# Group norm, a quantised 3x3 convolution and a residual on one core: 31 images in the direct form and 122 in the combined form in place of 75 and 82, with the engines' order taken from a timetable

## The chip, the cores and the metric

The kernel runs on one core of a Trainium2 chip. The time is the device time of one execution in microseconds (us). The core's engines each have a queue of their own and meet through semaphores: TensorE (PE: matmuls into PSUM; PEld is its weight load), VectorE (DVE), ScalarE (ACT), GpSimd (POOL) and SyncE (SP), which only issues DMAs here. GpSimd issues DMAs too. Each engine works strictly in the order in which its instructions were emitted.

## The reference

`x` has 160 images of 128 channels, 32 by 32, float32; `U` has five sets of weights (128 by 128 by 9). The reference, cut to what matters:

```
gn(x)  = (x - mean) / sqrt(var + 1e-5)          # per image and group of 4 channels
s1 = (max(U) - min(U)) / 3;  v1 = s1 * floor(U / s1)
s2 = s1 / 5;                 v2 = s2 * floor((U - v1) / s2)
w  = v1 + v2                                    # 5 sets
out = x + conv3x3(gn(x) of images 32n..32n+31, w[n], padding 1)   # n = 0..4
```

The normalised image is carried as two float16 parts, a high part and the rest (low part), and the weights, being small whole numbers after scaling, fit in float16.

## The kernel before, in words

One image fills the core's 128 partitions (a channel each) with 1,024 elements. Images are worked on in order, 0 to 159, and set `n` of the weights serves 32 of them. There are three forms of an image's convolution, counted here in matmuls of up to 512 columns, which is what TensorE spends:

- **Direct** (images 0 to 2): high and low part each go through 9 taps into 2 row parities, 36 matmuls.
- **Mixed** (75 images): the high part goes through the 9 taps for both parities (18 matmuls, `taps`). The low part is first turned on VectorE into sums and differences of row pairs (`combinations`, three operations), and then needs 12 matmuls (`product`): 30 in all.
- **Combined** (82 images): the sums and differences are built of the image itself into a wide tile `v` of 2,048 columns: on GpSimd the outer columns and the last quarter (`beside_pairs`), on VectorE the rest (`combine`, two operations). ScalarE scales it to the high part `vh`, VectorE makes the low part `vl` of 2,048 columns. Both go through `product`: 24 matmuls.

For mixed and combined images the sums of pairs come out of two passes, `m2` and `m1` (`sums_of_pairs`, 6 matmuls in a mixed image and 12 in a combined one, within the counts above). ScalarE copies `m2` out of PSUM (`leave`), VectorE makes both PSUM halves of the result from `m1` and `m2` (`pairs`, two operations), and the `main` matmuls add onto them. TensorE's order is: the sums of image i+1, then `main` of image i in two halves. There is one `m2` place, two `m1` places, and two pairs of result banks.

The result leaves PSUM by ScalarE (`sum<-eo`) and is added to the image in SBUF by an accumulating DMA that GpSimd issues (`accumulate`); for every eighth image and the last four VectorE does both in one operation (`by_hand`). SP stores two images at a time and loads the next two into the same place; there are 11 places of two images.

Statistics: for each image ScalarE runs two activations with accumulators (a sum, then a square about the mean, `measure`); eight images ride on VectorE instead (`BY_VECTOR`). For groups of images (2, 2, 4, 4, 4, 4, 4, then eight at a time) a float32 matmul averages over channel groups, VectorE forms the deviations, a second matmul averages them, ScalarE, GpSimd (a power) and VectorE finish the scale. From `z` on: a mixed image is normalised on GpSimd (`z`; the first of each group on ScalarE), cut to `hi` on ScalarE and to `lo` on VectorE.

The weights of sets 1 to 4 are quantised during the images before them, a third of a set (a column of taps) at a time: 14 VectorE operations of 384 elements a column (`quantise`, line 112 on), a transposing matmul and a ScalarE copy (`keep_taps`), and at the end sums of taps (`sums_of_set`).

The order is written out by hand in `run`: for each image a fixed list of calls, with a rule for every kind of image, measuring 14 images ahead and loading 18 ahead. GpSimd's operations get an extra wait for the last VectorE operation before `pairs`, so that they run while VectorE reads PSUM:

```
def combined(self, i):
    if i < self.STEADY or i >= self.imgs: return False
    if i < self.FIFTHS: return i % 2 == 1
    return (i - self.FIFTHS) % 5 % 2 == 0 if i < self.THIRDS else i % 3 != 1
```

Here `STEADY` is 7, `FIFTHS` 126 and `THIRDS` 146: every other image is combined at first, then three in five, at the end two in three.

Of the kernel before, what the change touches and what calls it, by code (L numbers as in the profile page):

```python
# [16 lines left out]
N_SETS = 5  # L17
# [13 lines left out]
WIDEST = 40.0  # L31


class Steps:
# [61 lines left out]
    def nearest(self, pool, v, parts, name, dt, by_scalar=False):  # L96

        tag = "m" if by_scalar else "nn"
        n = pool.tile(list(v.shape), dt, tag=tag, name=f"n{tag}_{name}")
        engine = self.nc.scalar.mul if by_scalar else self.nc.vector.tensor_scalar_mul  # L100
        return n, engine(n, v, parts[0])
# [13 lines left out]
    def quantise(self, pool, un, name, dt, by_scalar=False):  # L115
# [14 lines left out]
        nn, first = self.nearest(pool, rest, self.parts2, name + "_2", ints)  # L130
# [215 lines left out]
class Main:  # L346
# [24 lines left out]
    STAT_LEAD = 14  # L371
    LOAD_LEAD = 18
    STEADY = 7
    BY_VECTOR = (8, 10, 11, 14, 19, 24, 29, 34)
    FIFTHS = 126
    THIRDS = 146
# [9 lines left out]
    def __init__(self, tc, ctx, keep, x, u, out):  # L386
# [17 lines left out]
        self.xpool = pool("x", 11)  # L404
        self.zpool = pool("z", 3)
        self.parts = pool("parts", 5)
        self.rows = pool("rows", 4)
        self.wide = pool("wide", 2)
        self.wide_parts = pool("wide_parts", 3)
# [3 lines left out]
        self.small = pool("small", 3)  # L413
# [14 lines left out]
        self.sum = {}  # L428
        self.tables, self.wts, self.across = {}, {}, {}
        self.columns = []  # L430

        cuts = [0, 2, 4, 8, 12, 16, 20, *range(24, self.imgs + 1, 8)]
# [143 lines left out]
    def measure(self, i, stages=(0, 1)):  # L576
# [8 lines left out]
        for s in stages:  # L585
            junk = self.unread.tile([self.P, 1024], MM, tag="junk", name=f"junk{i}_{s}")
            (st.image_sum, st.image_square)[s](j, image, junk)

    def normalise(self, i):
# [3 lines left out]
        z = self.zpool.tile([self.P, 1024], F32, tag="z", name=f"z{i}")  # L593
# [11 lines left out]
    def combined(self, i):  # L605

        if i < self.STEADY or i >= self.imgs:
            return False

        if i < self.FIFTHS:  # L610
            return i % 2 == 1
        return (i - self.FIFTHS) % 5 % 2 == 0 if i < self.THIRDS else i % 3 != 1

    def by_scalar_too(self, i):

        return i < self.FIRST + 4 or i == self.groups[self.group_of[i]].start
# [21 lines left out]
    def combine(self, i):  # L638
# [4 lines left out]
        v, x, half = self.v[i], self.image(i), self.W // 2  # L643
# [11 lines left out]
    def beside_pairs(self, i, after):  # L655

        nc = self.nc
        if self.combined(i):
            self.v[i] = self.wide.tile([self.P, 2048], F32, tag="v", name=f"v{i}")
            self.after(self.outer_columns(i), after)  # L660
            even, odd = (self.image(i)[:, a::2] for a in range(2))
            ins = nc.gpsimd.tensor_sub(self.v[i][:, 1536:], odd, even)  # L662
        elif self.by_scalar_too(i):
            return
        else:
            st, j = self.column_of(i)
            z = self.z[i] = self.zpool.tile([self.P, 1024], F32, tag="z", name=f"z{i}")
            ins = nc.gpsimd.tensor_scalar(  # L668
                z, self.image(i), st.ngm[:, j], st.rstd[:, j], ALU.add, ALU.mult
            )  # L670
        self.after(ins, after)

    def after(self, ins, before):

        self.tc.add_manual_dep(
            ins.ins, before.ins.name,
# [44 lines left out]
    def taps(self, i, part, col, target, parities=(0, 1)):  # L721
# [7 lines left out]
        for k in self.KS:  # L729
            for a in parities:  # L730
# [7 lines left out]
                    start=(i < self.FIRST and col == self.COLS[0] and k == 1 and top == 0),  # L738
# [54 lines left out]
    def m1(self, i):  # L793
        return self.m1b if i % 2 else self.m1a
# [5 lines left out]
    def sums_of_pairs(self, i):  # L800

        for quarter, kind, target in (
            (3, self.DIFF, self.m2_ps), (2, self.SUM, self.m1(i))
        ):
            for step in self.KS:
                self.product(target, i, quarter, step, kind, start=step == self.KS[0])

    def conv(self, i, on_the_way):


        if self.FIRST < i < self.imgs - 1:
            self.sums_of_pairs(i + 1)
        if i == self.FIRST:
            self.main(i, 0)
            on_the_way(self.COLS[1])
            self.sums_of_pairs(i + 1)
            self.main(i, 1)
# [405 lines left out]
```

## Time and profile before

| | us |
|---|---|
| three runs | 978.17, 979.36, 985.92 (median 979.36) |
| the profiled execution | 982.18 |
| its span, first to last instruction | 980.5 |
| TensorE busy | 943.3 (96%) |
| VectorE busy | 913.8 (93%) |
| ScalarE busy | 833.4 (85%) |
| GpSimd busy | 353.5 (36%) |
| granted TensorE clock | 0.997 |

Busy time is the time in which at least one instruction of the engine was under way. The instructions of an engine overlap a little at their ends: an operation listed with 2.34 us lets the next one start after 2.26. A table by stage cuts the span into stretches and gives each engine's busy time in them; the difference to the length of the stretch is idle. The table of waits says who idled for whom.

### The profile page before, as it was taken

Reading aid. Unit: us, or ns where it says so; the run is one execution under the profiler, and the core shown is the slowest. Engines: PE = TensorE matmul, PEld = TensorE weight load, DVE = VectorE, ACT = ScalarE, POOL = GpSimd, SP = SyncE. Lnnn points to the kernel's source line nnn. Section 1 sums busy time; section 2 is a strip of 40 time slices with the busy share of each in tenths; the row PEclk is TensorE's granted clock in tenths of the full one; section 3 lists DMA queues with packets and bytes.
Section 4 is the critical chain, followed back from the end, with each engine's and each line's share of the span. In section 5 each row is a group of like instructions: output and inputs, shape, how many; then the busy total and the mean of one; then the engine's idle time right before and its main releaser. Section 6 shows DMA issues by size and latency. Waiting matters only on the chain.

```text
span 980.5 us, 13236 instructions
## 1 busy us (share of the span) xinstructions
PE 943.3 (96%) x4504; PEld 440.8 (45%) x4504; DVE 913.8 (93%) x1332; ACT 833.4 (85%) x1135; POOL 353.5 (36%) x441
## 2 busy tenths in 40 slices
PE   2899999999999999999999999999999999999997
PEld 1444444444444444444444444444444444444443
DVE  7999999998999999899999998799999998989995
ACT  5779889999999999889898989698989899898551
POOL 4353333343333333333343333233433434333530
PEclk9999999999999999999999999999999999999999
DMA  9627889999998888999998999998989989998774
GB/s 352 264 95 207 230 236 267 265 250 257 319 297 242 269 232 244 257 289 273 250 267 240 272 247 253 285 281 265 239 261 259 258 249 269 247 247 251 178 207 160
DMA packets 65117, 245.86 MB, mean 251 GB/s; under 512 B 5008, under 2 KB 5008, under 8 KB 65040
## 3 DMA queue, kind: packets, MB, share of 16 engines
q1 hardware_dynamic: 45312, 173.09, 49.4%
q0 software_dynamic: 19728, 71.84, 38.8%
q8 instruction: 37, 0.61, 0.2%
q14 instruction: 40, 0.33, 0.1%
HBM read 89.19 MB, written 83.89 MB: 177 GB/s over the span
## 4 chain that ended last, share of the span: by engine, by line
PE 74%; DVE 12%; DMA 6%; issue 4%; ACT 2%; POOL 2%; SPq 0%; DVEq 0%; POOLq 0%
PE eo L789 25%; PE eo L734 23%; PE m L789 12%; PE m1b L789 8%; PE m1a L789 5%; DMA out_dram<-xt 3%; DVE vl L690 2%; DVE v L644 1%; DMA u<-in_L_conv_U_dram 1%; DVE lo L697 1%; DVE eo L846 1%; DMA xt<-sum 1%; DMA range<-in_L_conv_U_dram 1%; DVE eo L848 1%; DVE v L651 1%
## 5 line engine op out<-in xcount | busy, mean ns | idle before, releaser
L734 PE MATMUL eo<-hi,wt 128*128 128x496 f16 (+2 forms) x1386 | 367.7, 375 | 0.7 <-ACT wt L527 0.7
L789 PEld LDWEIGHTS <-wt 128*128 128x128 f16 x1884 | 183.9, 99 | 216.1 <-DVE rows L719 5.2
L734 PEld LDWEIGHTS <-wt 128*128 128x128 f16 x1458 | 142.6, 99 | 163.7 <-ACT wt L527 1.4
L874 ACT COPY sum<-eo 128x1024 f32<-128x1024 f32 x137 | 143.1, 1045 | 63.2 <-PE eo L789 63.0
L690 DVE SCALAR_TENSOR_TENSOR vl<-v,rstd,vh 128x2048 f16<-128x2048 f32 x82 | 192.2, 2344 | 1.4 <-ACT vh L684 1.4
L789 PE MATMUL eo<-vh,wt 128*128 128x496 f16 (+1 forms) x492 | 185.0, 376 | 1.0 <-DVE eo L848 0.9
L789 PE MATMUL eo<-vl,wt 128*128 128x496 f16 (+1 forms) x492 | 184.9, 376 | 0.0
L684 ACT ACTIVATE vh<-v,rstd 128x2048 f16<-128x2048 f32 x82 | 164.1, 2001 | 17.1 <-DVE v L651 16.9
L209 ACT ACTIVATE junk<-xt,mv 128x1024 f16<-128x1024 f32 x152 | 174.3, 1147 | 0.1
L202 ACT ACTIVATE junk<-xt 128x1024 f16<-128x1024 f32 x152 | 160.6, 1057 | 15.2 <-DMA xt<-in_x_dram 11.6
L789 PE MATMUL eo<-rows,wt 128*128 128x496 f16 (+1 forms) x450 | 170.8, 380 | 0.0
L789 PEld LDWEIGHTS <-across 128*128 128x128 f16 x984 | 96.2, 98 | 116.0 <-issue 5.1
L668 POOL TENSOR_SCALAR z<-xt,ngm,rstd 128x1024 f32<-128x1024 f32 x53 | 62.8, 1184 | 232.3 <-DVE tt L109 39.6
L632 POOL TENSOR_SCALAR v<-xt,ngm 128x64 f32<-128x64 f32 x82 | 30.9, 377 | 257.1 <-issue 72.7
L897 POOL DMA_DIRECT2D xt<-sum x137 | 119.8, 878 | 4.4 <-ACT sum L874 3.1
L837 ACT ACTIVATE m<-m 128x512 f32<-128x512 f32 x157 | 94.0, 599 | 24.9 <-PE m L789 18.7
L644 DVE TENSOR_TENSOR v<-xt 128x960 f32<-128x960 f32 x82 | 106.2, 1295 | 2.8 <-POOL v L632 2.8
L789 PE MATMUL m<-vl,across 128*128 128x496 f16 (+1 forms) x246 | 92.1, 374 | 3.3 <-DVE vl L690 3.2
L697 DVE TENSOR_TENSOR lo<-z,hi 128x1024 f16<-128x1024 f32 x78 | 94.9, 1216 | 0.0
L789 PE MATMUL m<-vh,across 128*128 128x496 f16 (+1 forms) x246 | 92.1, 375 | 0.0
L662 POOL TENSOR_TENSOR v<-xt 128x512 f32<-128x512 f32 x82 | 84.8, 1034 | 0.0
L602 ACT CAST hi<-z 128x1024 f16<-128x1024 f32 x78 | 81.5, 1044 | 1.2 <-POOL z L668 0.5
(144 smaller groups left out, 1151.8 us busy)
## 6 DMA issues: line engine op xcount, KB each, us to landing
xt<-in_x_dram SPq DMA_DIRECT2D x78, 1024.0 KB, 7.0
out_dram<-xt SPq DMA_DIRECT2D x78, 1024.0 KB, 8.7
xt<-sum POOLq DMA_DIRECT2D x137, 512.0 KB, 7.2
u<-in_L_conv_U_dram SPq DMA_DIRECT2D x4, 576.0 KB, 9.7
xt<-in_x_dram SPq DMA_DIRECT2D x4, 512.0 KB, 9.9
range<-in_L_conv_U_dram SPq DMA_DIRECT2D x3, 576.0 KB, 8.1
out_dram<-xt SPq DMA_DIRECT2D x3, 512.0 KB, 2.7
u<-in_L_conv_U_dram SPq DMA_DIRECT2D x2, 288.0 KB, 3.0
```

What stands on the lines that cost most here:

```text
L202: self.nc.scalar.activation(junk, image, ACTF.Copy, scale=-1.0 / image.shape[1], accum_out=self.mv[:, j, 0:1],)
L209: self.nc.scalar.activation(junk, image, ACTF.Square, bias=self.mv[:, j, 0:1], accum_out=self.mv[:, j, 1:2],)
L644: nc.vector.tensor_tensor(self.view(v, 1, (511, 2), (half, H), (1, half - 1)), self.view(x, 1, (1, 2), (W, H), (2, half - 1)), self.view(x ...
L662: ins = nc.gpsimd.tensor_sub(self.v[i][:, 1536:], odd, even)
L684: self.nc.scalar.mul(vh, self.v[i], st.rstd[:, j])
L690: yield self.nc.vector.scalar_tensor_tensor(vl, self.v[i], st.rstd[:, j], self.hi[i], ALU.mult, ALU.subtract)
L697: self.nc.vector.tensor_sub(lo[:, 1 : self.H + 1, :].rearrange("p h w -> p (h w)"), self.z.pop(i), self.hi[i].rearrange("p h w -> p (h w)"),)
L734: nc.tensor.matmul(self.bank(target, a)[:, first:end, c0:c1], self.wts[n, col][:, k, :], tile[:, s0 : s0 + 2 * (end - first) - 1 : 2, c0 + ...
L789: self.nc.tensor.matmul(out, weights, moving, start=start and j == 0, stop=False, skip_group_check=True)
L837: self.nc.scalar.mul(m2, self.m2_ps, 0.5)
L874: nc.scalar.copy(self.as_banks(i, self.sum[i]), self.flat(i, eo))
L897: self.nc.gpsimd.dma_start(self.image(i), self.sum.pop(i), accum_op=ALU.add)
```

## The change

1. **Forms.** `FIFTHS` and `THIRDS` go. A new form, plain, is the direct form in the steady part: high and low part both go through `taps` (36 matmuls, no sums, no `pairs`). `PLAIN` are images 9, 13, 17, 22, 27, ..., 157, 31 in all. Images 3 to 6 stay mixed, and all others from 7 on, 122, are combined.
2. **Order.** From image 3 on nothing is written out by hand. `steady` describes every piece of work as a `Job` with an engine, a cost, what it needs, and how it is emitted. `Timetable` sets due times backwards from TensorE's order, plays the engines forward with the given costs, picks on VectorE and ScalarE the due job that is ready, and puts GpSimd's work beside `pairs` or `by_hand`. The instructions are then emitted by start time, so that each engine's order is the timetable's. A GpSimd operation beside `pairs` now waits for the VectorE instruction before the last one (`before_last`).
3. **Groups** of five images for the statistics from image 20 on, in place of four and eight.
4. **Places.** Three wide tiles in place of two, four `vh` in place of three; two `z` in place of three, four `hi` in place of five, ten places of two images in place of eleven. The unread output of the statistics becomes uint8 in place of float16.
5. **Smaller.** Of each column's 14 quantising operations two go from VectorE to ScalarE; the sums of taps that only mixed images use are not made for sets 1 to 4; `by_hand` is images 24, 34, ..., 154 and the last four; the load of set `n`'s weights (`n` from 2) may start 40 images before the set's first image, that is 8 images before the previous set begins, as soon as the place is free; its quantising starts ten images later (before, the load was issued at the previous set's first image and the quantising began two images later).

The diff, cut to its core:

```diff
-    STAT_LEAD = 14
-    LOAD_LEAD = 18
+    CHUNKS = 10
     STEADY = 7
-    FIFTHS = 126
-    THIRDS = 146
+    PLAIN = (9, 13, 17, *range(22, 160, 5))
+    HANDS = range(24, 156, 10)
...
-        self.xpool = pool("x", 11)
-        self.zpool = pool("z", 3)
-        self.parts = pool("parts", 5)
+        self.xpool = pool("x", self.CHUNKS)
+        self.zpool = pool("z", 2)
+        self.parts = pool("parts", 4)
-        self.wide = pool("wide", 2)
-        self.wide_parts = pool("wide_parts", 3)
+        self.wide = pool("wide", 3)
+        self.wide_parts = pool("wide_parts", 4)
...
-        cuts = [0, 2, 4, 8, 12, 16, 20, *range(24, self.imgs + 1, 8)]
+        cuts = [0, 2, 4, 8, 12, 16, *range(20, self.imgs + 1, 5)]
...
-            junk = self.unread.tile([self.P, 1024], MM, tag="junk", name=f"junk{i}_{s}")
+            junk = self.unread.tile([self.P, 1024], mybir.dt.uint8, tag="junk", name=f"junk{i}_{s}")
...
+    def before_last(self):
+        of_engine = (
+            i for i in reversed(self.nc.cur_bb.bb.instructions) if i.engine == self.vector_engine
+        )
+        next(of_engine)
+        return next(of_engine)
...
     def main(self, i, a, between=lambda: None):
+        if self.plain(i) and a == 0:
+            self.eo[i] = self.bank_pair(i)
...
-            self.product(to, i, a, step, 2 * a)
+            if self.plain(i):
+                self.taps(i, (self.los[i % len(self.los)], 1), step, self.eo[i], (a,))
+            else:
+                self.product(to, i, a, step, 2 * a)
...
+        for i in images:
+            comb, plain = self.combined(i), self.plain(i)
+            if comb:
+                beside[i] = add("t", "beside", 1.41, lambda i=i: self.differences(i))
+                wide[i] = add("combine", "vector", 1.73, lambda i=i: self.combine(i))
+                high[i] = add("vh", "scalar", 1.89, lambda i=i: self.high_combined(i), (beside[i], wide[i]))
+                low[i] = add("vl", "vector", 2.28, lambda i=i: last_of(self.low_combined(i)), (high[i],))
...
+            if not plain and i > first:
+                left[i] = add("leave", "scalar", 0.5, lambda i=i: self.leave(i), (m2[i],))
+                pairs[i] = add("pairs", "vector", 1.33, lambda i=i: self.pairs(i), (left[i], m1[i]))
+                pairs[i].window = True
...
+            if c >= loaded:
+                loads[c] = add("load", "queue", 10.0, lambda c=c: self.load(c), (stores.get(c - self.CHUNKS),))
...
+                one = add("sum", "scalar", 1.06, lambda i=i: self.measure(i, (0,)), (load,))
+                two = add("square", "scalar", 1.16, lambda i=i: self.measure(i, (1,)), (one,))
...
+                load = add("load u", "queue", 0.1, lambda n=n: self.load_set(n), (last_rest,), ready=at[use - 40])
...
+        done = table.run()
+        for job in done:
+            for other in job.with_it:
+                before = self.before_last()
+                for ins in other.emit():
+                    self.after(ins, before)
+            job.emit()
```

The heart of `Timetable.run`, for VectorE and ScalarE (`late` is a job's due time, `ready` the end of what it needs plus 0.14 us for a hop between engines):

```
for job in waiting[engine][:80]:
    at = self.ready(job)
    if at is None: continue
    if at <= now:
        if best is None or job.late < best.late: best = job
    elif at < now + self.SOON and (soon is None or job.late < soon.late):
        soon = job
if best and soon and soon.late < best.late and now + best.cost > soon.late:
    best = None          # wait for the more urgent one
```

## The prediction

> **What bounds the kernel now.** I read the page's busy shares first, then a table by stage, then the waits, then the chain that ended last. The shares:
>
> ```profile
> PE 943.3 (96%) x4504; PEld 440.8 (45%) x4504; DVE 913.8 (93%) x1332; ACT 833.4 (85%) x1135; POOL 353.5 (36%) x441
> ```
>
> Three engines are nearly full, so an average doesn't say which one ends last. The stages do (us, then each engine's busy time and count):
>
> ```profile
> 0.00:47.00 47.00, 25.70 (x122) 12.49 (x123) 40.71 (x78) 30.47 (x49) 17.77 (x38) 1.00 0.81 309
> 47.00:125.00 78.00, 75.57 (x364) 35.34 (x363) 75.52 (x135) 66.52 (x96) 31.21 (x45) 1.00 0.66 185
> 125.00:180.00 55.00, 51.11 (x246) 23.73 (x245) 54.16 (x86) 49.14 (x69) 21.46 (x29) 1.00 0.92 252
> 180.00:620.00 440.00, 440.00 (x2112) 206.27 (x2111) 417.64 (x602) 398.18 (x547) 157.98 (x183) 1.00 0.94 261
> 620.00:640.00 20.00, 17.80 (x80) 7.76 (x79) 13.95 (x26) 15.80 (x21) 4.20 (x5) 0.91 0.98 319
> 640.00:925.00 285.00, 284.82 (x1363) 133.13 (x1362) 270.35 (x365) 254.27 (x340) 108.05 (x126) 1.00 0.91 252
> ```
>
> The columns are TensorE, weight load, VectorE, ScalarE, GpSimd, clock, DMA. For 440 us TensorE is never idle, at full clock: there the time is its matmuls and nothing else. Its idle time is 21.3 before 47 us, 7.2 after its last matmul (at 973.3 of 980.5), and between them 2.43 + 3.89 + 2.20 + 0.18 = 8.7. So 943.3 + 21.3 + 7.2 + 8.7 = 980.5. From 125 to 180 VectorE is the bound (54.16 of 55). The hole at 620 is a late weight load, as the chain shows (start, length, what):
>
> ```profile
> 587.00 12.36 DMA out_dram<-xt
> ...
> 599.90 13.31 DMA out_dram<-xt
> ...
> 614.19 11.96 DMA u<-in_L_conv_U_dram
> ...
> 626.17 0.47 DVE nnn L101
> ```
>
> SP issued it behind two loads that had to wait for stores.
>
> **The change part by part.**
>
> *TensorE.* Combined, mixed and plain images need 24, 30 and 36 matmuls. Before: 82x24 + 75x30 + 3x36 = 4326. After: 122x24 + 4x30 + 34x36 = 4272. In the saturated stretch 2,112 records take 440 us; without the small ones, the long matmuls of both forms start 0.2115 us apart by the timeline. So 54 fewer give -11.4 us, all on the path. The groups become 34 from 24: ten more pairs of small float32 matmuls. A pair costs 0.24 us in the chain (0.12 for one, in two passes) and at most 0.56 by the timeline's 0.28 for one; I take 0.35, so +3.5 (2.4 to 5.6). TensorE's work becomes 935.4.
>
> *VectorE*, from these rows and their neighbours:
>
> ```profile
> L690 DVE SCALAR_TENSOR_TENSOR vl<-v,rstd,vh 128x2048 f16<-128x2048 f32 x82 | 192.2, 2344 | 1.4 <-ACT vh L684 1.4
> L644 DVE TENSOR_TENSOR v<-xt 128x960 f32<-128x960 f32 x82 | 106.2, 1295 | 2.8 <-POOL v L632 2.8
> L697 DVE TENSOR_TENSOR lo<-z,hi 128x1024 f16<-128x1024 f32 x78 | 94.9, 1216 | 0.0
> L684 ACT ACTIVATE vh<-v,rstd 128x2048 f16<-128x2048 f32 x82 | 164.1, 2001 | 17.1 <-DVE v L651 16.9
> ```
>
> Forty more combined images: 40x(1.295 + 0.741 + 2.344) = +175.2. Pairs 157 to 126, two operations of 0.69 and 0.70: -43.1. Low parts 78 to 38: -48.6. Combinations 75 to 4, three operations of 0.684 + 0.415 + 0.414: -107.4. Two fewer by hand (1.217): -2.4. Two quantising steps a column go to ScalarE, 12x(0.477 + 0.414): -10.7; tap sums, 12x0.346: -4.2. Twelve more groups in VectorE's seven small operations (1.19): +14.3. Sum -26.9, to 886.9, against TensorE's -7.9: relatively VectorE gains room.
>
> *ScalarE.* +40x2.001 = +80.0; `leave` -31x0.599 = -18.6; `hi` -40x1.044 = -41.8; copies out 2x1.045 = +2.1; `z` 25 to 7, -18x1.239 = -22.3; ten more small ones +1.7; the 24 quantising steps between 0.48 (a 384-element copy, L527) and 0.81 (the same multiply on ScalarE, L101), taken at 0.65: +15.6. Sum +16.7, to 850.1. The uint8 output has no row. Casts to float16 and copies to float32 take the same (1.044 and 1.045), which says nothing changes; the one int16 row (0.81 for 384 elements) says it could be slower, but that one also reads with a stride. I take 0 and keep 0.02 for a cost that would make ScalarE the bound outright.
>
> *GpSimd.* +40x1.411 - 22x1.184 + about 6 for power and accumulates: +36, to 390 of 970, free in sum. Its place is not: L644 takes 1.148 us alone and up to 1.987 where GpSimd's L662 is still under way, so a collision costs at most 0.84. With 122 such images after 82, 20 collisions more would cost 17 us of VectorE, inside the 26.9 it gains; nothing at the least. I take nothing. The Trainium skill, SBUF — State Buffer, section "Who interferes with whom", speaks against the change here: a VectorE instruction with two SBUF inputs and a GpSimd instruction that reads SBUF exclude each other, and the one that issues second waits for the whole of the first. As the new wait releases GpSimd one VectorE instruction earlier, it will often be blocked behind `vl`, which by the rule costs GpSimd only; an estimate by that page's rule, were GpSimd first each time, is 122 times a difference's 1.41 us, 172 us. The 1.987 agrees in kind.
>
> *DMA and SP.* The bytes stay, two accumulates more. In SP's order a load now stands behind the store 9 or 10 places back (11 before). ScalarE's order measures an image when the 13th before it has left PSUM (the 16th before), so from leaving to measuring of a place's old and new image there are 6 or 7 images, 34 us or more, where there were 5. Accumulate, store and load land in 7.2 + 8.7 + 7.0 = 22.9 at the medians; even with a load held back behind the next store's accumulate, it arrives. The wait behind any load is ScalarE's whole queue, and between 560 and 660 us it cost ScalarE 1.8 once. The weight load is asked for 8 images (45 us) ahead of the previous set's first image and some ten before its first use, in place of two images: the 2.2 at 620 goes.
>
> *What is left of the holes.* Counting start-to-start spacings of these rows over the new order in fives of images, TensorE needs about 28.1 us a five, VectorE 25.5 to 28.7 from image 10 to 130, ScalarE 24.2 to 29.8 (mean near 26.9). The first stage, images 10 to 30, has VectorE at 26.7, 28.5, 28.6, 28.2: better than 54.16 of 55, not free. I put 2 for the start (2.4), 2 for images 10 to 30 (3.9), 0 for 620, 2 for the rest: 6 in place of 8.7.
>
> **Sum.** -11.4 + 3.5 - 2.7 = -10.6: the profiled span goes from 980.5 to 969.9, its time from 982.18 to 971.6. That execution lies 2.8 above the median of 979.36, so the median goes to 968.8, called 969.
>
> **Rivals.**
>
> *The fives balance, the images don't.* `pairs` of an image can start only when its `m1` is through, about one image ahead of its `main`, so VectorE cannot work ahead on them. Where a by-hand image (1.15), a low part (1.14) and a group's seven operations (0.9) fall between two `pairs`, TensorE waits. At 0.4 us a five over 31 fives that is 12.4 more: 981. For it: VectorE has up to 28.7 of 28.1. Against it: before, at 98 to 99% in several stretches of 180 to 620, nothing was lost.
>
> *ScalarE becomes the bound* (the slower side). Its waits, in order, were:
>
> ```profile
> ACT sum L874 <- PE eo L789: 63.0, 50, 4.8
> ACT m L837 <- PE m L789: 18.7, 27, 7.0
> ACT vh L684 <- DVE v L651: 16.9, 16, 2.4
> ```
>
> 98.6 us, within 980.5 - 833.4 = 147.1 idle. If all of that stays, because each copy out still stands in line before its matmuls end, the span is 850.1 + 147.1 = 997.2, the time 996. It decides as soon as less than 27 us of the 98.6 go. Against it: they are waits of an engine that is early, and shrink when it is late.
>
> *The timetable removes all holes:* less than 2 us remain, 965 or a little under.
>
> *The change does not do what it says:* fewer matmuls are certain by count; that more than 54 x 0.2115 comes back as gaps is the two rivals above.
>
> **Numbers.** Holes of 2 to 9: 0.45, giving 965 to 972. Holes under 2: 0.11. The unbalanced images, 972 to 990: 0.25. ScalarE's bound: 0.17; uint8: 0.02. A measurement here tells about 1% from no change, that is 969.6 and 989.2. Faster: 0.11 + 0.35 = 0.46; within 1%: 0.10 + 0.20 = 0.30; slower 0.24. The range runs from 963 (holes near zero, small matmuls at their low price) to 996.
>
> **What would show it.** TensorE near 935 busy; the hole at 620 gone, those before 180 smaller; VectorE near 887; ScalarE near 850 with its wait on the result down from 63. Wrong, if TensorE waits in the steady part for `pairs` or `vl` (first rival), if those wait in turn for `vh` or `m` of ScalarE (second), if ScalarE waits on image loads, or if L377 and L384 exceed 1.06 and 1.15.

## The result

The changed kernel takes 993.0 us (median of four runs, 992.5 to 993.2), the kernel before in the same comparison 978.9 (978.2 to 985.9): a ratio of 1.0127, with a 95% interval of 1.0081 to 1.0173. The change makes the kernel slower by 1.3%, where I forecast 969. The executions of the kernel before scatter: in the four later comparisons their medians lie between 981.7 and 985.2, and the changed kernel, run once more beside one of them, is 0.7% slower. Ratios leave out executions that lie more than 1.5% above the fastest of the same kernel; the medians and ranges given here count all. The profiled execution took 992.5, with a span of 990.8.

### The profile after

The page's busy shares, and five of its costliest groups (busy time, mean ns of one, idle time before them and what ended most of it):

```profile
PE 936.0 (94%) x4490; PEld 438.0 (44%) x4490; DVE 930.6 (94%) x1183; ACT 857.6 (87%) x1120; POOL 613.6 (62%) x497
...
L817 POOL TENSOR_SCALAR v<-xt,ngm 128x64 f32<-128x64 f32 x122 | 208.5, 1709 | 180.2 <-issue 93.9
L885 DVE SCALAR_TENSOR_TENSOR vl<-v,rstd,vh 128x2048 f16<-128x2048 f32 x122 | 290.5, 2381 | 15.7 <-ACT vh L879 15.0
...
L377 ACT ACTIVATE junk<-xt 128x1024 uint8<-128x1024 f32 x152 | 160.9, 1059 | 25.1 <-DMA xt<-in_x_dram 23.6
...
L850 POOL TENSOR_TENSOR v<-xt 128x512 f32<-128x512 f32 x122 | 161.5, 1324 | 0.0
...
L829 DVE TENSOR_TENSOR v<-xt 128x960 f32<-128x960 f32 x122 | 155.5, 1275 | 0.7 <-POOL v L817 0.3
```

TensorE's 936.0 is the forecast's 935.4. ScalarE's 857.6 is near its 850.1. VectorE has 930.6 where I had 886.9, and GpSimd 613.6 where I had 390. The first group says where GpSimd's time went. The same operation on the page of the kernel before:

```profile
L632 POOL TENSOR_SCALAR v<-xt,ngm 128x64 f32<-128x64 f32 x82 | 30.9, 377 | 257.1 <-issue 72.7
...
L662 POOL TENSOR_TENSOR v<-xt 128x512 f32<-128x512 f32 x82 | 84.8, 1034 | 0.0
```

A copy of 64 columns took 0.38 us, and now takes 1.71 on average; the 512 columns took 1.03, and now 1.32. The work is the same: GpSimd stands still inside the instruction.

The table by stage, in the stretches of the prediction (length, then TensorE, weight load, VectorE, ScalarE and GpSimd busy, clock, DMA share, GB/s):

```profile
47.00:125.00 78.00, 72.67 (x357) 33.80 (x355) 74.58 (x126) 67.11 (x94) 38.53 (x44) 1.00 0.56 158
125.00:180.00 55.00, 50.89 (x240) 23.49 (x239) 52.39 (x70) 45.19 (x57) 35.60 (x27) 0.97 0.93 255
180.00:620.00 440.00, 428.38 (x2064) 200.36 (x2063) 430.00 (x529) 404.51 (x528) 294.15 (x218) 1.00 0.93 262
620.00:640.00 20.00, 20.00 (x99) 9.55 (x97) 18.40 (x23) 19.84 (x28) 10.10 (x8) 1.00 0.96 288
640.00:925.00 285.00, 279.74 (x1351) 131.74 (x1350) 271.75 (x320) 264.96 (x346) 194.68 (x146) 1.00 0.92 259
```

The 440 us in which TensorE was never idle now hold 11.6 us of holes, 640 to 925 holds 5.3, and only 620 to 640 is better. Length less TensorE's busy time gives, from 47 to 925 us, 5.33 + 4.11 + 11.62 + 0 + 5.26 = 26.3 us of holes (8.7 before, 6 forecast). So the span's excess over my 969.9, 20.9 us, is 20.3 of holes and 0.6 of TensorE work; the two ends are as long as I had them.

Below I count the holes in five stretches, 47 to 125, 125 to 230, 230 to 620, 620 to 860 and 860 to 925 us. Before: 2.4, 3.9, 0, 2.2, 0.1. After: 5.3, 7.4, 8.4, 5.3, 0.

Who waits, from the table of waits after 47 us (us in total, times, longest):

```profile
PEld L984 <- DVE eo L1032: 21.8, 22, 3.7
...
DVE vl L885 <- ACT vh L879: 15.0, 9, 4.0
ACT junk L377 <- DMA xt<-in_x_dram: 13.9, 6, 4.4
PE eo L984 <- DVE eo L1032: 13.7, 16, 3.2
```

TensorE waits for `pairs` (L1032) on VectorE, VectorE for `vh` on ScalarE, and ScalarE six times for an image's load. ScalarE's wait on the result (`sum`), 63.0 before, fell to 9.6. So all three engines are late now, one after another.

### The profile page after: what moved, and what is told of

Its sections match the earlier page's. It is cut to its first block, busy times and chain, and to the rows that moved or that the text cites. A ratio compares the mean times of both kernels' runs of the same rounds, so it can differ in the third digit from the quotient of the medians.

```text
span 990.8 us, 13088 instructions
## 1 busy us (share of the span) xinstructions
PE 936.0 (94%) x4490; PEld 438.0 (44%) x4490; DVE 930.6 (94%) x1183; ACT 857.6 (87%) x1120; POOL 613.6 (62%) x497
## 4 chain that ended last, share of the span: by engine, by line
PE 37%; DVE 31%; issue 11%; DMA 9%; ACT 8%; POOL 3%; SPq 0%; DVEq 0%; ACTq 0%; POOLq 0%
PE eo L984 14%; PE eo L929 9%; DVE vl L885 8%; PE m L984 7%; DMA xt<-in_x_dram 5%; DVE v L829 4%; DMA xt<-sum 4%; PE m1a L984 3%; PE m1b L984 3%; DVE v L836 3%; DVE eo L1030 3%; DVE eo L1032 2%; ACT junk L377 2%; ACT vh L879 2%; DVE lo L892 2%
## 5 line engine op out<-in xcount | busy, mean ns | idle before, releaser
L817 POOL TENSOR_SCALAR v<-xt,ngm 128x64 f32<-128x64 f32 x122 | 208.5, 1709 | 180.2 <-issue 93.9
L885 DVE SCALAR_TENSOR_TENSOR vl<-v,rstd,vh 128x2048 f16<-128x2048 f32 x122 | 290.5, 2381 | 15.7 <-ACT vh L879 15.0
L984 PE MATMUL eo<-vh,wt 128*128 128x512 f16 x732 | 275.2, 376 | 14.7 <-DVE eo L1032 13.7
L984 PE MATMUL eo<-vl,wt 128*128 128x512 f16 x732 | 274.9, 376 | 0.0
L984 PEld LDWEIGHTS <-wt 128*128 128x128 f16 x1512 | 145.8, 100 | 186.7 <-DVE eo L1032 21.8
L377 ACT ACTIVATE junk<-xt 128x1024 uint8<-128x1024 f32 x152 | 160.9, 1059 | 25.1 <-DMA xt<-in_x_dram 23.6
L929 PE MATMUL eo<-hi,wt 128*128 128x496 f16 (+3 forms) x666 | 176.6, 376 | 2.3 <-DVE eo L1032 1.6
L384 ACT ACTIVATE junk<-xt,mv 128x1024 uint8<-128x1024 f32 x152 | 174.4, 1147 | 3.1
L929 PE MATMUL eo<-lo,wt 128*128 128x496 f16 (+2 forms) x594 | 158.2, 378 | 0.0
L829 DVE TENSOR_TENSOR v<-xt 128x960 f32<-128x960 f32 x122 | 155.5, 1275 | 0.7 <-POOL v L817 0.3
L984 PE MATMUL m<-vh,across 128*128 128x512 f16 x366 | 137.1, 375 | 3.9 <-ACT m L1021 3.9
L984 PE MATMUL m<-vl,across 128*128 128x512 f16 x366 | 137.1, 375 | 0.0
```

The costliest lines, as they stand in the source:

```text
L377: self.nc.scalar.activation(junk, image, ACTF.Copy, scale=-1.0 / image.shape[1], accum_out=self.mv[:, j, 0:1],)
L384: self.nc.scalar.activation(junk, image, ACTF.Square, bias=self.mv[:, j, 0:1], accum_out=self.mv[:, j, 1:2],)
L817: return self.nc.gpsimd.tensor_scalar(self.view(self.v[i], 0, (512 + W // 2 - 1, 2), (W // 2, H)), self.view(self.image(i), 1, (W - 3, 2), ...
L829: nc.vector.tensor_tensor(self.view(v, 1, (511, 2), (half, H), (1, half - 1)), self.view(x, 1, (1, 2), (W, H), (2, half - 1)), self.view(x ...
L885: yield self.nc.vector.scalar_tensor_tensor(vl, self.v[i], st.rstd[:, j], self.hi[i], ALU.mult, ALU.subtract)
L929: nc.tensor.matmul(self.bank(target, a)[:, first:end, c0:c1], self.wts[n, col][:, k, :], tile[:, s0 : s0 + 2 * (end - first) - 1 : 2, c0 + ...
```

## The experiments

Unless said otherwise, an edit is made to the changed kernel, and nothing of the computation is left out. The changed kernel itself, run again with a later group of them, took 992.7 (989.9 to 997.9, ten runs; ratio 1.0071 [1.0036, 1.0105]):

> The changed kernel as it is, so that the three runs beside it are compared on one chip: 1 to 2% over the kernel before; holes of TensorE between 47 us and its last matmul 24 to 30 us, VectorE's stretch 48 to 53 us.

Its profiled execution (997.5) has holes of 5.7, 8.0, 8.1 and 8.2 us in the first four stretches. Holes of single profiles differ by about 3 us in a stretch, and I read them with that in mind. The "stretch" of VectorE's rows, of which the expectations speak, is the time by which its instructions are longer than others of their own kind: for each operation, the time of every instance above the median of its shorter half, summed. Over the whole span this gives 54.4 us in the changed kernel and 16.7 in the one before; the expectations' own count has 50.5 and 12.1.

### Which instruction releases GpSimd

```diff
     def before_last(self):
...
-        next(of_engine)
         return next(of_engine)
```

> Two theories of the loss. Port: GpSimd's reading operations and VectorE's operations block each other (VectorE's rows are 50.5 us longer than the same rows at their shortest half, against 12.1 before), and VectorE, full at 39.5 of 40 us, sets the steady part. ScalarE: it is nearly full, waits for late image loads (13.9 us after 60 us) and hands on vh and m2 late. Here the added wait of GpSimd's work beside pairs goes from the VectorE instruction before the last one to the last one. If the early release is what lets GpSimd in at the wrong place, VectorE's stretch falls below 30 us and the time to 980 to 986. If it is the work that the timetable puts beside no pairs at all (48 of 122 differences), which has no such wait, the 163 us for which L817 is blocked behind vl shrink a lot but VectorE's stretch stays at 40 or more and the time at 990 to 996. The ScalarE theory: no change, 991 to 995.

996.5 us (995.1 to 1000.2), ratio 1.0130 [1.0089, 1.0171]. VectorE's busy time stays at 935.1, the rows of VectorE that are longer than their own kind stay too, and the holes are 6.2, 7.2, 11.1, 6.4. GpSimd is under way for less (500.5 in place of 613.6; the median of its L817 is back at 0.38 us), and nobody gains. That is the second branch, half a microsecond above its range. The new, earlier release isn't the cause.

### GpSimd's differences read nothing

```diff
-        return self.nc.gpsimd.tensor_scalar(...)
+        return self.nc.gpsimd.memset(self.view(self.v[i], 0, ...), 0.0)
...
-        ... self.nc.gpsimd.tensor_sub(self.v[i][:, 1536:], odd, even)
+        ... self.nc.gpsimd.memset(self.v[i][:, 1536:], 0.0)
```

The differences and the outer columns are left out: zeros take their place. GpSimd still reads for the 31 normalised images and the powers.

> GpSimd's two operations for a combined image write zeros and read nothing, so the outer columns and the differences of the images are left out of the output; order, waits and places stay. Port theory: VectorE's stretch falls from 50.5 to under 12 us, TensorE's holes between 47 us and the last matmul from 26 to under 12, the time to 968 to 978. ScalarE theory: the stretch goes, but the holes stay over 20 and the time at 986 or more.

985.5 us (977.8 to 988.7), ratio 1.0026 [0.9994, 1.0059]. The page's busy shares:

```profile
PE 930.7 (95%) x4490; PEld 438.8 (45%) x4490; DVE 892.7 (91%) x1183; ACT 855.2 (87%) x1120; POOL 334.5 (34%) x497
```

VectorE has the same 1,183 instructions as the changed kernel and 37.9 us less busy time; 892.7 is 6 above what I had forecast for it. So my sum of VectorE's operations came out within 6 us, and 38 us of the excess are time in which its instructions are held by GpSimd's reads. GpSimd's own busy time falls by 279, of which the shorter work is some 70 (122 times 0.58). The holes after 230 us fall from 13.7 to 5.3; those before do not fall (5.6 and 10.0 in place of 5.3 and 7.4). So neither branch holds whole: the excess on VectorE goes, but 20.9 us of holes stay, and the time is at the edge of the ScalarE theory's range and far above the port theory's. The gain of some 7 us is not the collisions' alone either, since the edit also makes GpSimd's two operations 0.58 us shorter, and no run here separates the two.

One case as the timeline of the changed kernel shows it (start, length, engine; idle time before it and its end in brackets):

```profile
152.94 2.91 POOL L817 TENSOR_SCALAR v<-xt,ngm 128x64 f32<-128x64 f32 x1 [3.33 <-DVE v L829]
...
153.34 2.35 DVE L885 SCALAR_TENSOR_TENSOR vl<-v,rstd,vh 128x2048 f16<-128x2048 f32 x1
...
155.82 1.33 POOL L850 TENSOR_TENSOR v<-xt 128x512 f32<-128x512 f32 x1
...
156.29 1.28 DVE L284 SCALAR_TENSOR_TENSOR tt<-tt,s2r,nnn 128x384 f32<-128x384 f32 x1
...
157.18 2.00 ACT L879 ACTIVATE vh<-v,rstd 128x2048 f16<-128x2048 f32 x1 [0.65 <-POOL v L850]
...
157.77 1.04 POOL L850 TENSOR_TENSOR v<-xt 128x512 f32<-128x512 f32 x1
157.84 1.98 DVE L829 TENSOR_TENSOR v<-xt 128x960 f32<-128x960 f32 x1 [0.28 <-POOL v L817]
```

GpSimd's 64 columns end with `vl`, 2.9 us after their start. Then GpSimd's next read makes a quantising step on VectorE take 1.28, where the step of the same 384 elements just before it (L283) took 0.65, and the next one makes L829 take 1.98 where its typical time is 1.15. Between them ScalarE waits 0.65 for the late difference. TensorE has its longest hole, 3.2 us, at 164, before `main` of image 18. Collisions are not all of it: the timetable's own plan has a stall of TensorE of 2.3 us at this very place, and without the reads 1.3 us stay.

### The kernel before without the reads of GpSimd's differences

The same two edits in the kernel before; its differences are left out.

> The same as in the run without reads, on the kernel before: GpSimd's differences write zeros and read nothing, so they are left out of the output. Port theory: VectorE's 12.1 us of stretch go, but TensorE is the bound there (8.7 us of holes), so the time falls by 0 to 4 us, to 975 to 979. If the kernel before lost much to the port too, it falls by over 8.

976.4 us (974.7 to 992.1), ratio 0.9974 [0.9910, 1.0037]; the profiled execution 974.7, holes 1.4, 2.5, 0, 0, 0. VectorE's busy time falls from 913.8 to 903.0, by 10.8. The hand-written order pays 11 us of VectorE time for its collisions with the differences, the timetable's order 38.

### ScalarE with room

```diff
-            (st.image_sum, st.image_square)[s](j, image, junk)
+            (st.image_sum, st.image_square)[s](j, image[:, :512], junk[:, :512])
```

Half of the statistics' input is left out.

> ScalarE's statistics read 512 of an image's 1,024 columns, so they are those of half an image; order, waits and everything else stay. ScalarE's work falls by about 150 us of 858. ScalarE theory: the holes fall below 12 us, the time to 968 to 978. Port theory: VectorE stays at 39.5 of 40 us in the steady part, the holes over 18 us, the time at 986 to 993.

990.3 us (989.2 to 991.3), ratio 1.0068 [1.0036, 1.0099]. ScalarE has 121 us less work (736.4), 21.6 us of holes stay, and the kernel gains about 2.5, as the port theory said. (This run and the one without reads had no unchanged kernel beside them; their gains are differences to 992.7 from the next group.) So a ScalarE without room isn't a cause by itself. With both edits, the differences and half of the statistics' input left out:

> GpSimd's differences write zeros and read nothing, and ScalarE's statistics read half of an image: both are left out of the output, order and waits stay. Port alone took the holes between 230 and 860 us from 13.7 to 5.3, half statistics alone to 9.1. If the two are separate causes, nearly nothing is left there (under 2.5), and what stays is the start: 12 to 16 us of holes between 47 and 230 us, time 972 to 979. If what is left in the steady part is the order itself (an image's work between two pairs), 4 to 6 us stay there and the time is 976 to 982.

973.4 us (972.2 to 976.2), ratio 0.9899 [0.9831, 0.9967], holes 4.5, 5.1, 2.4, 0, 0. Together they gain 19.4 us, alone 7 and 2.5: with one of the engines relieved the other is the late one. In the run without reads alone, `vl` on VectorE waits 31.6 us for `vh` on ScalarE, 15.0 in the changed kernel:

```profile
L883 DVE SCALAR_TENSOR_TENSOR vl<-v,rstd,vh 128x2048 f16<-128x2048 f32 x122 | 287.2, 2354 | 32.5 <-ACT vh L877 31.6
```

### Loads

```diff
-                self.ov[n, :, b - NB + 1 : b + 1, :], self.chunks[i // NB]
+                self.ov[n, :, b - NB + 1 : b + 1, :512], self.chunks[i // NB][:, :, :512]
```

Half of the output of the paired stores is left out.

> Each store writes 512 of an image's 1,024 columns, so half of the output is left out and 40 MB of 247 MB of traffic; order and waits stay. If late image loads are a cause of their own, ScalarE's waits on them after 60 us (13.9 us in 6) fall under 4, the holes at 228, 425 and 845 us go, and the time falls by 4 to 8 us against the unchanged run beside it. If late loads only fall where ScalarE has time anyhow, it falls by less than 2 us.

983.9 us (981.8 to 986.4), ratio 0.9997 [0.9963, 1.0031]: 8.9 us less than the unchanged kernel of the same group. ScalarE's wait for loads after 47 us falls from 16.5 (first line, the unchanged kernel) to 1.0:

```profile
ACT junk L377 <- DMA xt<-in_x_dram: 16.5, 6, 6.6
```

```profile
ACT junk L377 <- DMA xt<-in_x_dram: 1.0, 1, 1.0
```

Its wait for accumulates, 9.2 in the unchanged kernel, goes as well, as accumulates land 6.0 us after their issue in place of 7.3. So the run relieves late transfers of both kinds, and the share of the loads alone stays open. In the transfers of the kernel before and of the changed one, from a store's issue to the landing of the load into its place took 15.8 us at the median of each, and an image was measured 6.3 us after landing at the median before and 7.1 after. But six of 70 loads after (two of 69 before) are followed by the measuring within 0.1 us of landing, that is, were waited for. The timetable plans 10 us each for the store and the load, and 0.9 for the accumulate ahead of them, which took 7.3 at the median to land.

All three together; half of the statistics' input, half of the paired stores' output and the differences are left out:

> The changed kernel with its three suspects relieved at once: GpSimd's differences become writes of zeros that read nothing, the two statistics passes read and write 512 of an image's 1,024 columns, and the stores of pairs of images write 512 of 1,024 columns (the differences, half of the statistics' input and half of the output are left out). Theory (the holes of the changed kernel come from collisions between GpSimd and VectorE, from late loads and from a ScalarE with no room, and the start is short of VectorE time): with the first and the second relieved the kernel took 973.4 and had 12 us of TensorE holes after 47 us; with late loads relieved too, the holes after 230 us fall to under 1.5, those of 47 to 230 us stay at 7 to 10, and the time is 967 to 972. Rival A (the loads cost nothing once ScalarE has room): 973 to 975, nothing changes. Rival B (the holes of the start come from late loads too): holes of 47 to 230 under 5, time under 967.

965.5 us (965.1 to 965.7), ratio 0.9834 [0.9774, 0.9895]. Busy shares, and two stretches of the table by stage:

```profile
PE 928.3 (96%) x4490; PEld 439.6 (46%) x4490; DVE 888.1 (92%) x1183; ACT 734.0 (76%) x1120; POOL 332.4 (35%) x497
```

```profile
47.00:230.00 183.00, 176.19 (x856) 83.12 (x855) 179.62 (x273) 141.05 (x216) 67.86 (x99) 1.00 0.74 194
230.00:925.00 695.00, 694.52 (x3367) 329.35 (x3366) 650.39 (x816) 558.73 (x846) 244.06 (x357) 1.00 0.84 219
```

From 230 us on TensorE idles 0.5 us in 695, and 6.8 between 47 and 230 (12.7 in the changed kernel). The time is 1.5 below the range of the theory, which holds otherwise: with collisions of the differences, late transfers and the full ScalarE taken away nothing is lost in the steady part. The holes left at the start stand beside a VectorE that is busy for 179.6 of 183 us.

### The forms of the kernel before in the timetable's order

```diff
-    PLAIN = (9, 13, 17, *range(22, 160, 5))
+    PLAIN = ()
...
-        return self.STEADY <= i < self.imgs and i not in self.PLAIN
+        if i < self.STEADY or i >= self.imgs:
+            return False
+
+        if i < 126:
+            return i % 2 == 1
+        return (i - 126) % 5 % 2 == 0 if i < 146 else i % 3 != 1
```

The places of `z` and `hi` follow the mixed images, and the sums of taps that these need are made again.

> Order, groups and places of the changed kernel, but the forms of the kernel before (82 combined, 75 mixed, no plain image): 54 more matmuls, 11.4 us. If the forms cause the loss (40 more images whose differences collide with VectorE), VectorE's stretch falls below 35 us, the holes below 14 us, and the time is 978 to 986, no more than 1% above the kernel before. If the order by the timetable, whatever it orders, causes it, the holes stay at 24 or more and the time is 994 to 1008.

1034.2 us (1031.7 to 1041.3), ratio 1.0525 [1.0441, 1.0608], holes 4.8, 6.0, 20.5, 10.6, 0. The kernel before has these forms too and 8.7 us of holes, in an order written by hand with other groups and places. ScalarE's wait for loads is 30.4 here. The time is far above both ranges. In the timetable's order the old forms cost 41 us more than the new ones, so more images in the combined form aren't what makes this order slow; the order with its groups and places is, 5% above the kernel before with the same forms. The new forms in an order written by hand are not tested, apart from the six images more below.

### Can the timetable be told?

```diff
-                loads[c] = add("load", "queue", 10.0, ...
+                loads[c] = add("load", "queue", 13.0, ...
```

> The changed kernel with one number of its timetable changed: a load is planned with 13 us in place of 10, so that measuring is placed where the image has really arrived. Everything is computed. Its own plan becomes 2.2 us longer. Theory (late loads cost some 9 us because ScalarE stands in line behind them): ScalarE's waits on loads after 47 us fall from 14 to under 5 us, and the time falls by 2 to 7 us, to 986 to 991. Rival (the plan had no room to measure later, so the wait only moves into ScalarE's order): loads' waits fall, the time stays at 991 to 996.

1002.9 us (1001.1 to 1003.9), ratio 1.0209 [1.0145, 1.0272]: neither branch. The waits for loads stay (16.7 in six) and TensorE's busy time rises to 942.3, which the last section explains. One number moves the whole order, and the plan's own time (2.2 us longer) says nothing of the 10 us it costs.

```diff
-    CHUNKS = 10
+    CHUNKS = 11
...
-        self.sums = pool("sums", 3)
+        self.sums = pool("sums", 2)
...
-            if i - 3 in out:
-                out[i].after(whole[i - 3])
+            if i - 2 in out:
+                out[i].after(whole[i - 2])
```

> The changed kernel with eleven places of two images in place of ten, as before the change; the room comes from the copies out of PSUM, two places in place of three. Everything is computed. The timetable plays it through anew and its own plan becomes 1.7 us shorter. Theory (ScalarE waits on loads because a place comes back one step too late): its waits on loads after 47 us fall from 14 to 17 us to under 5, and the time falls by 4 to 9 us, to 984 to 989. Rival (the transfers have no room: the DMA engines are 91 to 95% busy in the steady part, so loads are late with any number of places): the waits stay above 9 us and the time at 990 to 996. A price it may have: a copy out of PSUM waits for the accumulate two images back.

1036.4 us (1033.0 to 1039.0), ratio 1.0532 [1.0472, 1.0593]. No wait for a load is left in the table of waits, and the median image is measured 20.7 us after it landed. But the price that I had named ate it many times over:

```profile
ACT sum L1056 <- DMA xt<-sum: 70.9, 33, 6.6
```

The plan charges an accumulate 0.9 us, its issue; the place is free when it has landed, and with two places that is too late. As the kernel is slower, its loads also have more time, so the run doesn't prove that ten places alone make them late. With the 31 normalised images moved to VectorE as well (`Z_ENGINE = "vector"`):

> As the run before, and the 31 normalised images of the plain form come from VectorE in place of GpSimd. Everything is computed. The timetable then places 36 of 150 GpSimd jobs beside no pairs (64 of 183 in the run before), but its own plan is 11 us longer, as VectorE has 20 us more work. Theory (what the plan does not charge, collisions, is the larger part of the loss): rows of VectorE that are longer than their own kind fall from 50 to under 32 us, and the time is 978 to 988. Rival (VectorE's own work counts as the plan says): 990 to 1000.

1017.4 us (1015.3 to 1020.0), ratio 1.0359 [1.0301, 1.0417]. The stretch of VectorE's rows falls to 21.5 us (54.4 in the changed kernel) as the theory said, but ScalarE still waits 44.1 us for accumulates, and the time is above both ranges. It beats the run before by 19 us though VectorE has more work of its own. That fits collisions as the larger cost, but ScalarE's wait for accumulates is also 26.8 us shorter than in the run before, so it isn't shown; the sizes in the unchanged places stay open.

### The change's small parts in the hand-written order

```diff
-                if b == (2 if n == 0 else 0):
+                if n == 0 and b == 2:
                     self.load_set(n + 1)
...
-                    later = (s for col in self.COLS for s in self.make_column(n + 1, col))
+                    later = (s for col in self.COLS for s in self.make_column(n + 1, col, "later"))
...
                 if b == self.per_set - 4:
                     run(later)
+                    if n + 2 < N_SETS:
+                        self.load_set(n + 2)
```

> The kernel before, its order written out by hand, with two of the change's smaller parts alone: two of each column's 14 quantising steps on ScalarE for sets 1 to 4, and the weights of set n+2 loaded four images before set n ends (at once after the quantising of set n+1) in place of four images later. Everything is computed. Theory (the change's loss lies in the timetable's order, its smaller parts are good): the 2.2 us hole at 620 us goes, VectorE's busy time falls by about 9, and the time is 972 to 976 beside 978. Rival (a late weight load was not the cause of that hole, or ScalarE's steps hold up VectorE's): 978 to 982.

Its four executions lie far apart, 985.4 to 1007.3, all above both ranges; ratio 1.0160 [1.0044, 1.0276], from 985.4 and 990.4. In the profiled one (985.4) the hole at 626 us is gone, and new ones stand at 125 to 230 (5.2 in place of 3.9) and at 447 to 508 us (2.4 in three). With 88 combined images in place of 82 on top (`FIFTHS` 81, `THIRDS` 111):

> As the run before, and the hand-written order takes three combined images in five from image 81 on and two in three from 111 on (126 and 146 before): 88 combined in place of 82, 36 matmuls fewer. Everything is computed. Theory (in the hand-written order VectorE's place for six more combined images is paid by the quantising steps that ScalarE took over): TensorE's work 7.6 us less, holes up by at most 4, time 966 to 972, faster than both kernels. Rival (VectorE or ScalarE at 98 to 99% of the stretch has no room): the 7.6 come back as holes, 974 to 980.

990.5 us (986.9 to 996.5), ratio 1.0086 [1.0046, 1.0125]: holes 1.6, 5.2, 4.7, 8.9, 0.5, in sum 12 us more than before, so the 36 matmuls (7.6 us) and more came back as holes, and the time is above both ranges. The hand-written order with these small parts has no room for them either. With the weight load alone moved, quantising as before:

> The kernel before with one edit: the weights of set n+2 are loaded four images before set n ends in place of four images later; all 14 quantising steps stay on VectorE. Everything is computed. Theory (the hole of 2.0 us at 626 us comes from the late weight load, and TensorE's clock of 0.5 to 0.7 for some 4 us behind it costs 1.6 more; in the run with the small parts the new holes at 500 to 508 us came from ScalarE's steps): hole and clock dip are gone, no new ones come, 974.5 to 977 beside 978 to 979. Rival (the earlier load pushes image loads back and the holes at 500 to 508 us come from it): 978 to 985, with those holes there again.

982.8 us (977.4 to 998.2, twelve runs) beside 981.7, ratio 1.0008 [0.9972, 1.0044]: no difference in time that can be told. In the profiled execution (977.9) TensorE's holes from 230 to 860 us, 2.2 in the kernel before, are gone, and none stands at 500 to 508:

```profile
230.00:620.00 390.00, 390.00 (x1871) 182.81 (x1870) 370.00 (x530) 353.75 (x489) 137.59 (x160) 1.00 0.94 264
620.00:860.00 240.00, 240.00 (x1154) 112.77 (x1153) 228.58 (x323) 218.31 (x300) 89.37 (x104) 1.00 0.94 268
```

So the late weight load made that hole, and the new ones of the run with both parts came with the quantising steps on ScalarE, as far as one profile of each tells. No kernel that computes everything beat the kernel before by more than its runs vary.

## Why the prediction was wrong, step by step

- **TensorE's work, right.** 54 matmuls fewer and ten more groups: 935.4 forecast, 936.0 measured.
- **The hole at 620, right in cause.** It is gone, and the run with the early weight load shows the cause alone. Its size in the profile was more than 2.2: see the last section.
- **VectorE's own work, near in sum, by luck; the collisions, wrong.** "I take nothing" is the step that failed: the collisions that I put at nothing held VectorE for 38 us more. Without the differences' reads 20.9 us of holes stay of 26.3, and some 7 of the 24 us that I missed by go. The sum of 886.9 stands beside 892.7, 890.1 and 888.1 in the three profiles of the changed kernel without the differences' reads. Luck is in it: my price of 1.295 for L644 held the old order's collisions, and the same operation takes 1.179 on average without the reads, 14 us less for 122 images; what else the sum misses goes the other way. With the differences' reads left out of both kernels, VectorE falls from 903.0 to 892.7, by 10.3 and not by my 26.9, and TensorE by 7 to 11: the room that VectorE was to gain was hardly there, even ahead of the collisions. I had bounded the collisions by "20 collisions more would cost 17 us", scaling the old order's collisions by the number of images. But in the old order GpSimd's operations were tied to run beside VectorE's reads of PSUM, image by image. The timetable, by its own count when it lays out the order, leaves 67 of 183 GpSimd jobs beside no such stretch and charges VectorE 0.5 us for each in its plan. That is 33.5 us, close to the 38 measured, and it stood in the kernel that I was to forecast. L817 takes 2.3 us at the median in the changed kernel, 0.38 before: being held up is the rule and no accident of a few.
- **The rule that spoke against the change.** I quoted the Trainium skill, SBUF — State Buffer, "Who interferes with whom", and left it out of the sum. The runs agree with it in both halves: the small GpSimd copy is blocked behind `vl` (1.71 us on average for 0.38), VectorE's two-input operations behind GpSimd (L829 up to 2.0 for 1.15), and GpSimd instructions that only write take 38 us of the collisions away. Its other half, that only the side that issues second pays, I had used to call the wait GpSimd's alone; a chain of both kinds in turn is what the timeline shows.
- **"Even with a load held back behind the next store's accumulate, it arrives", wrong for six loads.** The medians I added up (22.9 us against 34) were right at the median; the late ones are the tail. Half the stores' bytes took these waits and those for accumulates away and 8.9 us off the time.
- **ScalarE as the bound, wrong as a rival by itself.** Half its statistics gave 2.5 us; it becomes the next late engine only after VectorE is relieved.
- **"The fives balance, the images don't" came nearest.** It named `pairs` arriving late, and TensorE does wait for L1032 (13.7 us, and the weight load in front 21.8). It took the cause to be the order of VectorE's own operations, at 12.4 us of holes, and left out held-up ones. The plan, below, speaks for a part of it.
- **The holes term, wrong.** This is the term of the sum that carries the miss: 6 forecast, 26.3 measured: 12.7 to 230 us (I put 2 and 2), 13.7 after it (I put 0 and 2). I could have asked the plan. `Timetable` notes each stall of TensorE while it lays out the order (its list `stalls`); they add up to 13.4 us from image 3 on, 7.3 in the plan's first 160 us and 6.1 later, with 2.3 before image 18 and 2.2 before image 23. In the profile the holes before these two images are 3.2 (ending at 164) and 1.7 (at 196). So about half of the holes was planned, collisions charged at 0.5 us included; the rest came on top. In the steady part 0.5 is left when all three are relieved, so the three together are enough to explain it, though that run also leaves out work. Of the start, 6.8 us stay when all three are relieved, beside a VectorE 98% busy, 2.4 of them before images 18 and 23, where the plan has its two longest stalls. How much of the rest each of the three causes has can't be told apart, since the gains of the single edits (7, 2.5, 9) and of the pair (19.4) don't add.
- **The uint8 output, right:** 1.06 and 1.15 us, as before.

## What to carry to other kernels

Where an edit lets a planner place an engine's work, read the planner's own stalls and charges before forecasting: this one had 13.4 us of stalls and 33.5 us of collisions in its plan. And cost an operation beside the instructions it will really meet: the durations of the old order, which kept collisions low by hand, are not the durations of the new one. In this kernel, with three engines from 85 to 96% busy, the matmuls saved came back as holes, and relieving one engine showed a fraction of the loss. In a plan that lays out an order, charge a transfer until it has landed and not until it was issued.

## What the runs showed of the hardware that I had not expected

A hole of TensorE can cost more than its length. In the table by stage, in steps of 2 us behind the hole that ends at 628.0 us in the kernel before (2.0 us long), and behind the one that ends at 164.2 in the changed kernel (3.2):

```profile
628.20:630.20 2.00, 1.81 (x7) 0.52 (x6) 1.97 (x4) 0.88 (x2) 1.50 (x2) 0.69 0.96 395
630.20:632.20 2.00, 2.00 (x6) 0.76 (x5) 1.97 (x7) 1.90 (x3) 0.50 (x1) 0.50 0.53 107
```

```profile
164.20:166.20 2.00, 2.00 (x5) 0.68 (x6) 1.97 (x8) 1.19 (x3) 0.68 (x1) 0.50 1.04 225
166.20:168.20 2.00, 2.00 (x10) 1.02 (x9) 2.00 (x2) 1.21 (x2) 2.00 (x2) 0.79 1.07 287
```

The clock is at 0.50 for a while, and five or six matmuls run in 2 us in place of ten to twelve. Over the 5 us behind such a hole the clock is 0.66 to 0.73 in nearly all cases, that is 1.4 to 1.7 us lost. I looked at all holes from 1.4 us between 47 us and the last matmul in the seventeen profiles. None of the 41 from 1.4 to 1.9 us was followed by half clock, 14 of the 25 from 2.0 to 2.8 us were, and 15 of the 16 from 3.1 us on. The exception, of 3.2 us, is the hole at 163 in the second profile of the changed kernel, the same place as the 3.2 us hole shown above. So the length alone does not decide, and what else does stays open. The run with later loads in the plan has four such holes, the changed kernel one, and its TensorE is busy for 6.3 us more with the same matmuls, of which three such spells more, at 1.4 to 1.7 us, are about 5. The hole at 626 in the kernel before thus cost its profile 3.7 us and not the 2.2 of my sum, though the medians of the run with the early weight load don't show a gain; and the one at 164 in the changed kernel took 1.4 back. The Trainium skill, TensorE: Matmul & The Clock Gate, "Part 1", speaks of half rate after an idle window of about 3.4 us; here a hole of 2.0 us was enough in some places, and the measurement decides.
